# Cross-attention on one core: score tiles of 308, 154 and 154 columns become 234, 234 and 156, and ScalarE writes a second copy of some queries

## The chip, the cores and the metric

One NeuronCore of a Trainium2 chip runs the program. The metric is the time of one execution on the device in microseconds (us), as the median of several; lower is better. The engines are TensorE (PE, with its weight loads shown as PEld), VectorE (DVE), ScalarE (ACT), GpSimd (POOL) and SyncE (SP), which here only issues DMAs. They run side by side, each its own list of instructions in order, and wait for each other through semaphores.

## What is computed

`x` is (32, 512, 640) in fp32, `ctx` is (32, 77, 1024). The reference, cut to what matters (the other key and value weights see empty slices, since all 77 context rows are text):

```
q = heads(x @ to_q_w)            # 20 heads of 32
k, v = heads(ctx @ to_k_w), heads(ctx @ to_v_w)
p = softmax(q @ k.T / sqrt(32))  # 512 x 77 per head
out = merge(p @ v) @ to_out_w + to_out_b + x
```

## The kernel before

**Tiling.** A batch's 640 query columns are five chunks of 128, so a chunk holds four heads of 32 rows. One chunk of one batch is an *item*; there are 32 x 5 = 160. An item's 512 queries are four tiles of 128. Products are made in float32r in three passes: each operand is split into a high part (a cast) and a low part (the rest), and high x high, high x low and low x high are added up in PSUM.

**An item's steps**, each named by one letter in the tables that set the order: `q` (`queries`, 15 matmuls of 512 columns into the one PSUM bank `pq`), `Q` (`high_query`: ScalarE casts `pq` into `qt[:, 0]`), `g` (`low_query`: VectorE subtracts, from `pq` again), `k` (`copy_query`: GpSimd moves rows of `qt` to other partitions), `s` (`score_tile`: three matmuls into one of three `sc` banks), `m` (VectorE: maximum of each head), `e` (`exps`: four exponentials with sums on ScalarE), `N` (normalize, GpSimd), `z` (32x32 block transpose, VectorE), `w` and `d` (out to DRAM and back, which completes the transpose), `c`, `R`, `l` (split of the probabilities), `v` (six matmuls with the values into the one bank pair `pa`), `A`, `a`, `h`, `L` (halves added, split again), `p` (projection, 24 matmuls of 320 columns per item), `f`, `o` (residual added, stored). Loads have `u`: `uk` keys, `uv` values, `ux` and `ur` the input.

**Scores.** A chunk's four heads need twelve products of 32 rows (three for each head) and a matmul takes 128 rows, so three matmuls do it with block-diagonal keys. Before, the first has the high queries of all four heads against 4 x 77 = 308 columns; the second and third have a pair of heads each, 154 columns: low queries against high keys in one half of the rows, high queries (moved there by GpSimd) against low keys in the other. So `qt` holds three stationary tiles `qt[:, 0..2]`. The keys lie in `kb` in four blocks of 154 columns per chunk; SP loads eight pieces per batch and group of chunks (group 0 holds chunks 0 to 2, group 1 chunks 3 and 4), and GpSimd copies two half-blocks (`copy_half_keys`, token `K`) to make the 308-column operand.

**Order.** Nothing is scheduled by the compiler. After a stage that makes all keys and values for 32 x 77 context rows (to about 256 us in the trace), three tables of tokens give the order: `FILL` (the rest of that stage together with batches 0 and 1), `PLAN` (once for each of batches 2 to 30, 29 times) and `LAST_` (batch 31 and the end). A token is chunk digit, letter, argument; every engine runs its share of the tokens in the table's order. Steps of different items are interleaved: the queries of item n+1 stand beside the scores of n and the values of n-4.

**What the change touches**: `score_tile` (L563 to L584), `score_max`, `exps`, `load_keys` and `copy_half_keys` (L503 to L519), `high_query`, `copy_query`, `low_query` (L777 to L787), and the three tables.

## Time and profile before

| | us |
|---|---|
| three timed runs | 1857.3, 1859.1, 1859.61 (median 1859.1) |
| the profiled execution, first to last instruction (the page gives it no other time) | 1856.5 |
| PE busy | 1842.4, 99% of the span |
| ACT busy | 1527.2, 82% |
| DVE busy | 1563.4, 84% |
| POOL busy | 1303.9, 70% |
| DMA: share of the 16 engines on SP's queue | 84.5% |

The shares are means over stages. Up to 256 us only the key and value stage runs, where ACT and POOL have little to do; in the stage of the tables all of them are busier. In a matmul's row the end is modelled and successive matmuls overlap, so what a matmul costs is read from start to start and not from its duration.

### The profile page before, as it was taken

Reading aid. Unit: us, or ns where it says so; the run is one execution under the profiler, and the core shown is the slowest. Engines: PE = TensorE matmul, PEld = TensorE weight load, DVE = VectorE, ACT = ScalarE, POOL = GpSimd, SP = SyncE. Lnnn points to the kernel's source line nnn. Section 1 sums busy time; section 2 is a strip of 40 time slices with the busy share of each in tenths; the row PEclk is TensorE's granted clock in tenths of the full one; section 3 lists DMA queues with packets and bytes.
Section 4 is the critical chain, followed back from the end, with each engine's and each line's share of the span. In section 5 each row is a group of like instructions: output and inputs, shape, how many; then the busy total and the mean of one; then the engine's idle time right before and its main releaser. Section 6 shows DMA issues by size and latency. Waiting matters only on the chain.

```text
span 1856.5 us, 37492 instructions
## 1 busy us (share of the span) xinstructions
PE 1842.4 (99%) x10332; PEld 1655.7 (89%) x10332; DVE 1563.4 (84%) x2502; ACT 1527.2 (82%) x6218; POOL 1303.9 (70%) x1120
## 2 busy tenths in 40 slices
PE   9999999999999999999999999999999999999998
PEld 7888897889999999999999999999999999999998
DVE  5445458899999999999999999999999999999996
ACT  3233248899999999999999999999999999999984
POOL 1100268778788788778778877887778878877874
PEclk9999999999999999999999999999999999999999
DMA  9889779998998898888998888998889988888875
GB/s 188 199 198 249 184 193 256 254 242 235 247 240 243 240 238 232 242 235 236 238 244 237 234 243 237 244 238 237 235 234 244 244 241 236 237 232 243 228 228 187
DMA packets 563296, 431.37 MB, mean 232 GB/s; under 512 B 191120, under 2 KB 471120, under 8 KB 563088
## 3 DMA queue, kind: packets, MB, share of 16 engines
q1 hardware_dynamic: 558192, 413.16, 84.5%
q0 software_dynamic: 4800, 15.65, 2.7%
q8 instruction: 85, 1.39, 0.3%
q14 instruction: 123, 1.01, 0.2%
q10 hardware_dynamic: 96, 0.16, 0.0%
HBM read 247.17 MB, written 181.64 MB: 231 GB/s over the span
## 4 chain that ended last, share of the span: by engine, by line
PE 93%; DMA 4%; SPq 1%; DVE 1%; ACT 1%; issue 0%; POOL 0%; DVEq 0%; ACTq 0%; POOLq 0%
PE po L750 29%; PE pq L542 28%; PE pa L694 12%; PE sc L577 11%; PE pv L204 7%; PE pk L204 6%; DMA pd<-z 1%; DMA cs<-in_ctx_dram 1%; DMA xr<-in_x_dram 1%; DMA wo_s<-wo_dram 0%; DMA wraw<-in_L_xattn_to_v_w_dram 0%; DMA xs<-in_x_dram 0%; DMA wraw<-in_L_xattn_to_k_w_dram 0%; ACT pn L602 0%; DMA raw<-pd 0%
## 5 line engine op out<-in xcount | busy, mean ns | idle before, releaser
L602 ACT ACTIVATE pn<-sc,nm 128x77 f32<-128x77 f32 x2560 | 797.1, 343 | 36.0 <-DVE nm L588 29.6
L750 PE MATMUL po<-wo_s,at 128*128 128x320 f32 x3840 | 707.2, 310 | 0.1
L750 PEld LDWEIGHTS po<-wo_s,at 128*128 128x128 f32 x3840 | 619.7, 188 | 41.1 <-DVE xr L765 0.6
L542 PE MATMUL pq<-xt,wq_s 128*128 128x512 f32 x2400 | 596.7, 394 | 2.9 <-ACT pp L661 1.9
L602 ACT ACTIVATION_READ_ACCUMULATOR pn<-sc,nm 128x1 f32 x2560 | 567.5, 222 | 0.0
L542 PEld LDWEIGHTS pq<-xt,wq_s 128*128 128x128 f32 x2400 | 436.7, 188 | 82.5 <-ACT pp L661 2.1
L617 POOL TENSOR_TENSOR pn<-pn,rs 128x1232 f32<-128x1232 f32 x160 | 389.4, 2434 | 94.0 <-DVE rs L612 90.0
L694 PE MATMUL pa<-pp,vb 128*128 128x512 f32 x960 | 340.9, 403 | 4.1 <-DVE at L731 3.3
L577 PEld LDWEIGHTS sc<-kb,qt 128*128 128x128 f32 x1920 | 302.9, 188 | 14.4 <-ACT pn L602 1.8
L588 DVE TENSOR_REDUCE nm<-sc 128x4 f32<-128x308 f32 x640 | 295.0, 466 | 21.6 <-PE sc L577 16.7
L577 PE MATMUL sc<-kb,qt 128*128 128x154 f32 (+1 forms) x1920 | 301.9, 274 | 0.9 <-ACT pn L602 0.9
L783 POOL CAST qt<-qt 64x512 fp32r<-64x512 f32 x320 | 196.9, 615 | 139.5 <-ACT qt L779 124.4
L712 DVE TENSOR_TENSOR pa<-pa,aw 64x512 f32<-64x512 f32 x320 | 222.3, 695 | 50.4 <-ACT aw L708 43.2
L679 POOL TENSOR_TENSOR pp<-raw,pp 64x512 fp32r<-64x512 f32 x160 | 207.0, 1294 | 66.9 <-ACT pp L661 53.5
L624 DVE STREAM_TRANSPOSE z<-pn 128x1280 f32<-128x1280 f32 x160 | 241.2, 1507 | 8.8 <-DMA pd<-z 3.4
L708 ACT COPY aw<-pa 64x1024 f32<-64x1024 f32 x160 | 162.2, 1014 | 85.0 <-PE pa L694 83.9
L787 DVE TENSOR_TENSOR qt<-pq,qt 64x512 fp32r<-64x512 f32 x320 | 216.8, 678 | 13.9 <-ACT qt L779 9.0
L320 POOL TENSOR_TENSOR xt<-xs,xt 128x512 fp32r<-128x512 f32 x160 | 204.6, 1305 | 20.8 <-ACT xt L316 15.8
L743 POOL TENSOR_TENSOR xr<-xr,bias 128x640 f32<-128x640 f32 x128 | 202.3, 1581 | 13.1 <-issue 3.5
L672 DVE TENSOR_TENSOR pp<-raw,pp 128x1024 fp32r<-128x1024 f32 x160 | 195.7, 1223 | 0.0
L694 PEld LDWEIGHTS pa<-pp,vb 128*128 128x128 f32 x960 | 173.8, 189 | 15.1 <-DVE pp L672 2.3
L663 ACT CAST pp<-raw 128x1024 fp32r<-128x1024 f32 x160 | 168.1, 1051 | 0.7 <-DMA raw<-pd 0.7
(46 smaller groups left out, 1584.2 us busy)
## 6 DMA issues: line engine op xcount, KB each, us to landing
pd<-z SPq DMA_DIRECT2D x640, 160.0 KB, 3.4
raw<-pd SPq DMA_DIRECT2D x160, 512.0 KB, 4.5
xr<-in_x_dram SPq DMA_DIRECT2D x128, 320.0 KB, 3.9
out_dram<-xr SPq DMA_DIRECT2D x127, 320.0 KB, 3.7
xs<-in_x_dram SPq DMA_DIRECT2D x124, 320.0 KB, 5.8
raw<-pd SPq DMA_DIRECT2D x160, 128.0 KB, 4.2
v_dram<-vs SPq DMA_DIRECT2D x80, 192.0 KB, 4.0
k_dram<-ks POOLq DMA_DIRECT2D x20, 512.0 KB, 4.2
```

Of the source, the lines that this page charges most:

```text
L204: nc.tensor.matmul(held[j][:, :gn], w[:, k, a, :], cts[g, k][:, c, :gn], start=(k == 0 and n == 0), stop=(k == NK - 1 and n == 2),)
L542: nc.tensor.matmul(pqs[n], wq_s[:, k, a, j * P : (j + 1) * P], xts[b, k][:, c, :], start=(k == 0 and m == 0), stop=(k == NC_ - 1 and m == 2),)
L577: nc.tensor.matmul(sc[:, cols], qt[:, m, t * P : (t + 1) * P], keys_, start=(m == 0), stop=(m == 2),)
L588: nc.vector.tensor_reduce(nm, sc[:, :KCOLS].rearrange("p (h k) -> p h k", k=NKEY), AX.X, ALU.max, negate=True)
L602: nc.scalar.activation(pnb[n % 2][:, at, :NKEY], sc[:, i * NKEY : (i + 1) * NKEY], AF.Exp, bias=nm[:, i : i + 1], accum_out=sms[n][:, at : ...
L617: nc.gpsimd.tensor_tensor(pf, pf, rs.unsqueeze(2).to_broadcast([P, NQ * HPC, NKEY]), ALU.mult)
L624: nc.vector.transpose(z.rearrange("p b t j -> p t b j"), pn.rearrange("p (t h) k -> p t (h k)", t=NQ).rearrange("p t (b i) -> p t b i", i=Q),)
L679: nc.gpsimd.tensor_tensor(pp[64:, 4, :], raw[:64, 2, :], pp[:64, 4, :].bitcast(F32), ALU.subtract)
L694: nc.tensor.matmul(pas[n][:, p, :], vb[:, p, t, :], pp[:, c, :], start=(c == p), stop=(c == p + 2),)
L712: nc.vector.tensor_tensor(pa[64 * p : 64 * p + 64, 0], pa[:64, p], aw[:, p], ALU.add)
L750: nc.tensor.matmul(pos[b, t, h][:, :HALF], ats[b * NC_ + j][:, a, t * P : (t + 1) * P], wos[0][:, j, c, h * HALF : (h + 1) * HALF], start= ...
L787: nc.vector.tensor_tensor(qt[rows, 1 + w, :], pqs[n][rows], qt[rows, 0, :].bitcast(F32), ALU.subtract)
```

## The change

The twelve products of a chunk are packed evenly: the heads stand in the order 2, 0, 1, 3 in the score bank, each in a block of 78 columns (77 keys and a spare), and the three matmuls cover three blocks (2, 0, 1), three blocks (0, 1, 3) and two blocks (2 and 3, which are the first and the last). So the widths are 234, 234 and 156, 624 columns in place of 616, and the third matmul writes two runs that do not adjoin.

```diff
+KBLK = NKEY + 1
+ORDER = (2, 0, 1, 3)
+WIDTHS = (3 * KBLK, 3 * KBLK, 2 * KBLK)
...
+COPIES = ((1, 0, 0, 0, P), (2, 0, 0, 64, 64), (1, 64, 2, 0, Q))
+LOWS = ((2, 0, 0, P), (0, 96, 32, Q), (1, 64, 0, Q), (2, 64, 64, 64))
...
     def score_tile(n, t):
...
-        for m, (cols, keys_) in enumerate(
-            (
-                (slice(0, KCOLS), kb[:, 0::3, jg]),
-                (slice(0, half), kb[:, 1, jg]),
-                (slice(half, KCOLS), kb[:, 2, jg]),
-            )
-        ):
+        blocks = score_blocks(sc)
+        for m, heads in enumerate((blocks[:, 0:3], blocks[:, 1:4], blocks[:, 0::3])):
+            c0 = keys_at(nj, m) + (j - j0) * WIDTHS[m]
             nc.tensor.matmul(
-                sc[:, cols],
+                heads,
                 qt[:, m, t * P : (t + 1) * P],
-                keys_,
+                kb[:, c0 : c0 + WIDTHS[m]].rearrange("p (h k) -> p h k", k=KBLK),
...
-    def high_query(n):
+    def high_query(n, m=0):
         open_first()
-        nc.scalar.copy(qts[n % 2][:, 0, :], pqs[n])
+        nc.scalar.copy(qts[n % 2][:, m, :], pqs[n])
 
     def copy_query(n, w):
-        qt, half = qts[n % 2], (slice(0, 64), slice(64, P))
-        nc.gpsimd.tensor_copy(qt[half[1 - w], 1 + w, :], qt[half[w], 0, :].bitcast(F32))
+        qt, (m1, r1, m0, r0, rn) = qts[n % 2], COPIES[w]
+        nc.gpsimd.tensor_copy(qt[r1 : r1 + rn, m1, :], qt[r0 : r0 + rn, m0, :].bitcast(F32))
 
     def low_query(n, w):
-        qt, rows = qts[n % 2], slice(64 * w, 64 * w + 64)
-        nc.vector.tensor_tensor(qt[rows, 1 + w, :], pqs[n][rows], qt[rows, 0, :].bitcast(F32), ALU.subtract)
+        qt, (m1, r1, r0, rn) = qts[n % 2], LOWS[w]
+        rows = slice(r0, r0 + rn)
+        nc.vector.tensor_tensor(
+            qt[r1 : r1 + rn, m1, :], pqs[n][rows], qt[rows, 0, :].bitcast(F32), ALU.subtract
+        )
...
-        elif op == "K":
-            copy_half_keys(*arg)
+        elif op == "B":
+            high_query(n + 1, 1)
```

**Queries.** The first stationary tile is all high queries but for rows 96 to 127, which become the low queries of head 1 (`g1`, 32 rows). The second is all high queries but for rows 64 to 95, the low queries of head 0. The third has the high queries of heads 2 and 3 in rows 0 to 63 (`k1`) and low queries below. `k1` reads the rows that `g1` overwrites, so `g1` has to come after it, and `g1` is now the last reader of `pq`. There are two ways to fill the second and third tile. In most items of `PLAN`: `k0` (GpSimd copies all 128 rows of high queries), `g0` (VectorE, all 128 low rows into the third tile), `k2` (GpSimd takes 32 low rows from there), `k1`, `g1`. In `FILL`, `LAST_` and, for `k0` alone, one item of `PLAN` in five: token `B`, in which ScalarE casts `pq` a second time, into the second tile; in `FILL` and `LAST_` VectorE then makes the low rows in three subtractions (`g3`, `g2`, `g1`), and GpSimd is left with `k1`. The item behind `PLAN`'s token 3 has `k0`, `k1` and the three subtractions.

**Keys.** GpSimd's copies (`K`) go. SP loads ten pieces per batch and group in place of eight; two of the ten carry both the high and the low part.

```diff
-    def load_keys(b, g, heads=range(HPC), parts=(0, 1)):
...
-                    nc.sync.dma_start(kb[rows, 1 + i // 2, :, half], src[own, part])
...
+    def load_head_keys(b, g, piece):
+        nj = GROUPS[g][1]
+        i, part, quad, m, block = KEYS_OF[piece]
...
+        nc.sync.dma_start(
+            dst[:, c0 : c0 + nn * w].rearrange("p (r k) -> p r k", k=w)[:, :, :NKEY],
+            src[:, n0 : n0 + nn, b * NKEY : (b + 1) * NKEY].bitcast(F32),
+        )
```

**Order.** `FILL` and `LAST_` keep their old order with the new tokens in the old places; `PLAN` is another order altogether. Two lines of it, the start:

```diff
     PLAN = (
-        "1uv10 0r 0e0 0s2 0ux3 0g0 0N 0v0 1uv15 0v1 0m1 0v2 0f10 0p16 1uv11 0e1 0v4 0g1 0uk120 0p17 0v3 "
+        "0r 0v0 0v1 1uv10 0uk12 1uv16 0g0 0m1 0v2 0s2 0m2 0v3 0f10 0ux3 0v4 1uv15 0k0 0p16 0e0 1uv14 0k2 "
```

On TensorE, in the first batches of `PLAN`, two score tiles stand next to each other behind a projection (`po`) and are followed by another. Before:

```order
L750 MATMUL po<-wo_s,at_2694 128x320 x3
L577 MATMUL sc<-kb_1753,qt_1920 128x308
L577 MATMUL sc<-kb_1753,qt_1920 128x154 x2
L577 MATMUL sc<-kb_1753,qt_1920 128x308
L577 MATMUL sc<-kb_1753,qt_1920 128x154 x2
L750 MATMUL po<-wo_s,at_2689 128x320 x3
```

The same engine after, with the same surroundings (`128x2x78` is the third matmul, two runs of 78 columns):

```order
L745 MATMUL po<-wo_s,at_2698 128x320 x3
L577 MATMUL sc<-kb_1753,qt_1921 128x234 x2
L577 MATMUL sc<-kb_1753,qt_1921 128x2x78
L577 MATMUL sc<-kb_1753,qt_1921 128x234 x2
L577 MATMUL sc<-kb_1753,qt_1921 128x2x78
L745 MATMUL po<-wo_s,at_2699 128x320 x3
```

Each tile keeps three matmuls; their widths are what moved.

On GpSimd, the part of a `PLAN` batch that ends with the normalize (`pn`), last probabilities (`pp`) and low inputs (`xt`) ahead of the fourth item's query copies. Before:

```order
L617 TENSOR_TENSOR pn_1921<-pn_1921,rs 128x16x77
L679 TENSOR_TENSOR pp<-raw,pp 64x512
L320 TENSOR_TENSOR xt<-xs,xt 128x512
L783 CAST qt_1919<-qt_1919 64x512 x2
L320 TENSOR_TENSOR xt<-xs,xt 128x512 x4
L679 TENSOR_TENSOR pp<-raw,pp 64x512
L617 TENSOR_TENSOR pn_1922<-pn_1922,rs 128x16x77
L743 TENSOR_TENSOR xr<-xr,bias 128x640
L783 CAST qt_1920<-qt_1920 64x512
L519 CAST kb_1753<-kb_1753 64x462 x2
L783 CAST qt_1920<-qt_1920 64x512
```

After:

```order
L612 TENSOR_TENSOR pn_1923<-pn_1923,rs 128x16x77
L674 TENSOR_TENSOR pp<-raw,pp 64x512
L345 TENSOR_TENSOR xt<-xs,xt 128x512
L778 CAST qt_1921<-qt_1921 128x512
L778 CAST qt_1921<-qt_1921 64x512
L345 TENSOR_TENSOR xt<-xs,xt 128x512 x3
L738 TENSOR_TENSOR xr<-xr,bias 128x640
L674 TENSOR_TENSOR pp<-raw,pp 64x512
L778 CAST qt_1920<-qt_1920 128x512
L778 CAST qt_1920<-qt_1920 32x512
L778 CAST qt_1920<-qt_1920 64x512
```

The copies of keys are gone, the fifth item has three query copies where it had two, and the copies stand in the order `k0`, `k2`, `k1`.

On ScalarE, the start of `FILL`'s attention part, where the first items' queries are cast between other casts of the key stage. Before:

```order
L225 CAST ks<-pk 128x416
L779 CAST qt_1919<-pq 128x512
L316 CAST xt<-xs 128x512
L225 CAST ks<-pk 128x416 x2
L779 CAST qt_1920<-pq 128x512
```

After:

```order
L250 CAST ks<-pk 128x416
L774 CAST qt_1920<-pq 128x512 x2
L341 CAST xt<-xs 128x512
L250 CAST ks<-pk 128x416 x2
L774 CAST qt_1921<-pq 128x512 x2
```

Every cast of `pq` is there twice, one behind the other, and the exponentials that follow stand behind both.

More of the change, by code (lines that the diff above doesn't have):

```diff
@@ L452, in open_small @@
             small = ctx.enter_context(tc.tile_pool(name="small", bufs=1, reuse_waits="tile"))
-            kbs.append(small.tile([P, 4, GROUPS[0][1], KCOLS // 2], FPR, name="kb0"))
+            kbs.append(small.tile([P, keys_width(GROUPS[0][1])], FPR, name="kb0"))
     def open_first():
@@ L548, in queries, with score_blocks @@
                 )
-    def split_q(n):
-        qt, pq = qts[n % 2], pqs.pop(n)
-        nc.scalar.copy(qt[:, 0, :], pq)
-        lower, upper = slice(0, 64), slice(64, P)
-        halves = ((lower, upper), (upper, lower))
-        for w, (r, other) in enumerate(halves):
-            nc.gpsimd.tensor_copy(qt[other, 1 + w, :], qt[r, 0, :].bitcast(F32))
-        for w, (r, other) in enumerate(halves):
-            nc.vector.tensor_tensor(
-                qt[r, 1 + w, :], pq[r], qt[r, 0, :].bitcast(F32), ALU.subtract
-            )
+    def score_blocks(sc):
+        return sc[:, : HPC * KBLK].rearrange("p (h k) -> p h k", k=KBLK)
     def score_tile(n, t):
@@ L599, in exps @@
             sms[n] = small.tile([P, NQ * HPC], F32, tag="sm", name="sm", bufs=2)
-        for i in range(HPC):
-            at = t * HPC + i
+        for i, head in enumerate(ORDER):
+            at = t * HPC + head
             nc.scalar.activation(
                 pnb[n % 2][:, at, :NKEY],
-                sc[:, i * NKEY : (i + 1) * NKEY],
+                sc[:, i * KBLK : i * KBLK + NKEY],
                 AF.Exp,
```

52 lines of the change are left out of this document (26 added, 26 removed), and 164 rows, old and new, of tables (FILL, LAST_, PLAN).

## The prediction

> **What bounds the kernel now.** I read the page's shares and chain first, then the stretches of the span, then single rows of TensorE around one score tile. The page:
>
> ```profile
> span 1856.5 us, 37492 instructions
> PE 1842.4 (99%) x10332; PEld 1655.7 (89%) x10332; DVE 1563.4 (84%) x2502; ACT 1527.2 (82%) x6218; POOL 1303.9 (70%) x1120
> PE 93%; DMA 4%; SPq 1%; DVE 1%; ACT 1%; issue 0%; POOL 0%; DVEq 0%; ACTq 0%; POOLq 0%
> ```
>
> TensorE carries 93% of the chain that ended last. The shares are means, so the stretches (each: length, then busy us and count of PE, PEld, DVE, ACT, POOL; then clock, DMA share, GB/s):
>
> ```profile
> 260.00:340.00 80.00, 74.99 (x389) 65.31 (x389) 61.64 (x98) 68.25 (x307) 67.19 (x69) 1.00 0.89 237
> 310.00:330.00 20.00, 16.91 (x82) 13.18 (x80) 16.44 (x26) 19.90 (x93) 15.36 (x15) 1.00 0.97 304
> 370.00:390.00 20.00, 19.37 (x110) 17.10 (x110) 18.60 (x28) 19.02 (x73) 16.65 (x14) 1.00 0.84 231
> 1140.00:1240.00 100.00, 100.00 (x584) 91.04 (x583) 91.86 (x147) 92.14 (x386) 80.52 (x70) 1.00 0.90 239
> 1740.00:1857.00 117.00, 111.10 (x664) 101.75 (x662) 91.86 (x146) 84.74 (x320) 75.29 (x57) 1.00 0.70 208
> ```
>
> In the steady stretch (1140 to 1240, all of it PLAN) TensorE never stands; VectorE, ScalarE and the DMAs follow at about 92, 92 and 90 in 100. A batch has 285 matmuls (75 queries, 120 projections, 30 values, 60 scores), so it lasts 285/584 x 100 = 48.8 us. Only in FILL does TensorE stand: ScalarE is busy 19.90 of 20 at 310 to 330, and 5.0 us of TensorE are lost between 260 and 340. So in PLAN a shorter matmul stream is a shorter batch; in FILL more work on ScalarE is more time.
>
> A busy TensorE hides what its matmuls wait for. One score tile, in single rows (start, duration), read in narrow windows; PEld are the weight loads:
>
> ```profile
> 1000.15 1.48 PE L750 MATMUL po<-wo_s,at 128*128 128x320 f32 x9
> 1001.47 0.49 PE L577 MATMUL sc<-kb,qt 128*128 128x308 f32 x3
> ...
> 1001.47 0.33 PEld L577 LDWEIGHTS sc<-kb,qt 128*128 128x128 f32 x2
> 1001.61 0.19 PEld L577 LDWEIGHTS sc<-kb,qt 128*128 128x128 f32 x1
> 1001.72 0.19 PEld L694 LDWEIGHTS pa<-pp,vb 128*128 128x128 f32 x1
> 1001.83 0.19 PEld L750 LDWEIGHTS po<-wo_s,at 128*128 128x128 f32 x1
> ...
> 1001.60 0.35 PE L577 MATMUL sc<-kb,qt 128*128 128x154 f32 x2
> 1001.67 0.28 PE L577 MATMUL sc<-kb,qt 128*128 128x154 f32 x1
> ...
> 1006.61 3.65 PE L542 MATMUL pq<-xt,wq_s 128*128 128x512 f32 x15
> 1010.10 0.60 PE L750 MATMUL po<-wo_s,at 128*128 128x320 f32 x3
> ```
>
> The load for the second matmul starts with the first matmul (1001.47), the next at 1001.61 with the second, and then loads follow each other by 0.11, whether the matmul between them is long or not. So a load takes 0.11 and there is one spare place for weights: a matmul of 154 columns streams in 0.07 (1001.60 to 1001.67) but costs 0.11, because the weights of the next one are not there. From load to load the tile costs 0.14 + 0.11 + 0.11 = 0.36 us (1001.47 to 1001.83). Long matmuls cover their loads: nine of 320 columns take 1.32, 0.147 each, fifteen of 512 take 3.49, 0.233 each.
>
> **The change part by part.** *Widths.* Between 320 and 512 columns a column costs (0.233 - 0.147)/192 = 0.00045 us, so 234 columns take 0.147 - 86 x 0.00045 = 0.108, just what a load takes (0.11). 156 columns stream in about 0.07 and are bound by the load. The tile then costs 0.11 + 0.11 + 0.11 = 0.33, 0.03 less, though it has eight columns more. Bounds: not under 0.33, since no loads stand closer; not over 0.14 + 0.14 + 0.11 = 0.39, since 234 columns can't take longer than the 308 do. I take 0.33, the interpolation's value; 0.345 if load and stream, now equally long, miss each other by 0.007 twice. PLAN has 29 x 20 = 580 tiles: 580 x 0.03 = 17.4 us.
>
> The Trainium skill (TensorE: Matmul & The Clock Gate, "LDWEIGHTS (loading the stationary operand)" and "Back-to-back issue gap") gives a load 128/1.2 = 107 ns and a matmul N/2.4 + 2.5 ns, which makes the tile 131 + 107 + 107 = 345 ns before and 3 x 107 = 321 after, 24 ns less. By that estimate PLAN would gain 13.9 us; the trace agrees on the load (0.11) and has the 308 columns at 0.14.
>
> *ScalarE, VectorE, GpSimd in PLAN.* The prices:
>
> ```profile
> L779 ACT CAST qt<-pq 128x512 fp32r<-128x512 f32 x123 | 73.1, 594 | 0.4
> L787 DVE TENSOR_TENSOR qt<-pq,qt 64x512 fp32r<-64x512 f32 x246 | 166.4, 677 | 3.7
> L731 DVE TENSOR_TENSOR at<-pa,at 128x512 fp32r<-128x512 f32 x123 | 84.8, 690 | 34.0 <-ACT at L726 32.2
> L617 POOL TENSOR_TENSOR pn<-pn,rs 128x1232 f32<-128x1232 f32 x123 | 299.3, 2433 | 66.6 <-DVE rs L612 63.0 <-DMA pd<-z 3.5
> L679 POOL TENSOR_TENSOR pp<-raw,pp 64x512 fp32r<-64x512 f32 x123 | 159.2, 1295 | 48.8 <-ACT pp L661 43.1
> L320 POOL TENSOR_TENSOR xt<-xs,xt 128x512 fp32r<-128x512 f32 x120 | 152.4, 1298 | 3.8
> L783 POOL CAST qt<-qt 64x512 fp32r<-64x512 f32 x246 | 150.3, 611 | 108.2 <-ACT qt L779 96.5
> L519 POOL CAST kb<-kb 64x308 fp32r<-64x308 f32 (+1 forms) x98 | 49.6, 506 | 6.5 <-DMA kb<-k_dram 0.7
> ```
>
> 64 or 128 partitions cost the same on both engines (677 against 690, 1295 against 1298), so I price every subtraction at 0.68 and every query copy at 0.61, whatever its rows. ScalarE gets one cast per batch, 0.59; VectorE eleven subtractions in place of ten, 0.68; GpSimd thirteen query copies in place of ten and no key copies, 3 x 0.61 - 4 x 0.51 = -0.2. In a batch that shrinks from 48.8 to 48.2 ScalarE then has 0.921 x 48.8 + 0.6 = 45.6 us of work and VectorE 0.919 x 48.8 + 0.7 = 45.5, 94 to 95%. Both stay under TensorE, so I charge nothing; the cover is the 2.6 us that is left, and it is thinner.
>
> *The wait that is new.* `pq` is one bank; the next item's queries wait for its last reader. That was a subtraction behind the cast. Now it is `g1`, behind `k1` on GpSimd, mostly behind `k0` and `k2`: cast, copy, copy, copy, subtraction, 0.59 + 3 x 0.61 + 0.68 = 3.1 us. While `g1` waits, VectorE's later maxima and transposes stand behind it. The shortest cover in the new table lies between the token `3q4` and the token `4q0`: six projection steps, six value matmuls and a score tile, 6 x 3 x 0.147 + 6 x 0.233 + 0.33 = 4.4 us. There the chain is without `k2`, 0.59 + 2 x 0.61 + 0.68 = 2.5, so 1.9 are left. I take no stall.
>
> *SP and the DMAs.* Four loads more per batch; two of each ten are of double size:
>
> ```profile
> 1002.90 0.43 SPq L512 DMA_DIRECT2D kb<-k_dram  x1
> ...
> kb<-k_dram SPq DMA_DIRECT2D x256, 28.9 KB, 3.0
> ...
> kb<-k_dram SPq DMA_DIRECT2D x256, 19.2 KB, 3.2
> ```
>
> 4 x 0.43 = 1.7 us more of SP's queue, which issues some 74 in 48.8 us, and 4 x (28.9 + 19.2) = 192 KB more, 0.8 us at 239 GB/s: the DMA share goes from 0.90 to about 0.93. In the new table the last keys of a batch (`3uk07`) stand behind the store `4o0`, which waits for the projection step `4p8`. From there to the first score that needs them (`5s0`) TensorE has five projection steps, five value matmuls, two score tiles and five query steps, 5 x 0.44 + 5 x 0.233 + 2 x 0.33 + 5 x 0.70 = 7.5 us, against 3.0 for landing. Nothing charged.
>
> *FILL and LAST.* Here ScalarE gets a cast (0.59) and VectorE a subtraction (0.68) per item, on an old order. Eleven items in FILL: at worst all of it in series, 11 x 1.27 = 14; at best nothing. TensorE stands only in about 100 of FILL's 150 us, some six items: I charge the cast there, 6 x 0.59 = 3.6, less 40 x 0.03 = 1.2 gained: +2.4. In LAST ScalarE waits for the value matmuls often enough to hide it:
>
> ```profile
> ACT aw L708 <- PE pa L694: 14.3, 9, 3.4
> ```
>
> That is 14.3 us in nine waits from 1745 on, against 3 x 0.59; zero there, and up to +2.
>
> *Sum*: 1856.5 - 17.4 + 2.4 = 1841.5 for the profiled execution. The median of the runs stands 2.6 above that span (1859.1), so 1844.
>
> **The rivals.** *Half the gain*: the tie of load and stream costs 0.007 per wide matmul (tile 0.345), or the thinner cover of ScalarE and VectorE lets a wait through. 580 x 0.015 = 8.7 gained, 2.4 + 2.6 added: 1852.8. For it: two engines at 95%; against: at 92% not one wait reaches TensorE in the steady stretch.
>
> *The split output is slow*: the third matmul writes two runs of 78 columns, which no row shows. If that halves its rate it streams in 2 x 0.07 = 0.14, the tile is 0.11 + 0.11 + 0.14 = 0.36, nothing is gained and FILL's 3.6 stay: 1862.7. It decides once the third matmul takes over 0.11, a loss of the whole 0.03 at 0.14. Against: the 308 columns read their keys in two runs and keep to the line (0.147 - 12 x 0.00045 = 0.142). The Trainium skill (PSUM — Partial Sum Buffer, "Specifications (TRN2)") says that any non-contiguous access pattern slows matmuls significantly; by that rule this rival holds. No run here shows it for an output.
>
> *`pq` comes free late*, the rival on the slower side: in GpSimd's order a normalize (2.43), a `pp` (1.30) and an `xt` (1.30) stand right ahead of the fourth item's copies. If GpSimd reaches `k0` more than 1.9 us after the cast, the queries of token `4q0` wait. One `xt` too late in each batch is 29 x 1.30 = 37.7: 1856.5 - 17.4 + 2.4 + 37.7 + 2.6 = 1881.8; from 0.55 us per batch on the gain is gone. For it: GpSimd is the one engine that `pq` did not depend on. Against: its idle time ahead of its query copies is mostly waiting for the cast (96.5 of 108.2 us), so it is early there.
>
> *No effect*: the loads of the neighbours, not the tile, set the 0.36, and TensorE's stream is as long as before: 1859 to 1861.
>
> **How the numbers follow.** Forecast 0.64 (1837 to 1850, its own range), half the gain 0.17, split output 0.07, late `pq` 0.08, no effect 0.04. A measurement here tells 0.2% (3.7 us: 1855.4 to 1862.8) from no change. Faster: the forecast and most of the second, 0.79. Same: no effect, half of the split output and the rest of the second, 0.09. Slower: late `pq` and the other half, 0.12. The range for 8 in 10 holds the first two: from 1837 (rows are rounded to 0.01, so a tile may gain 0.035; 640 x 0.035 = 22.4 with nothing lost in FILL: 1856.5 - 22.4 + 2.6 = 1836.7) to 1858, the far side of the second.
>
> **What would show it.** In the profile after, weight loads around a score tile at steps of 0.11, none of 0.14, and 1140 to 1240 with about 591 matmuls (584 x 48.8/48.2) and a full TensorE. A step of 0.14 behind the third matmul is the split output. A wait of `pq`'s matmuls for VectorE's `qt` in every batch is the late bank. The stretch 260 to 390 should be some 2 us longer. I am wrong if PLAN's batch is not near 48.2 us, and in the mechanism if it is but the steps of the loads are not 0.11.

## The result and the profile after

The kernel after takes 1921.6 us (median of 4 runs, 1920.6 to 1922.0) against 1858.7 for the kernel before: a ratio of 1.0338, 95% interval 1.0323 to 1.0352. It is 63 us slower where 15 less were forecast, outside the range and beyond every rival's time. The page of the profiled execution, the lines that answer to those of before:

```profile
span 1918.8 us, 37409 instructions
PE 1852.6 (97%) x10332; PEld 1640.0 (85%) x10332; DVE 1614.2 (84%) x2546; ACT 1554.3 (81%) x6261; POOL 1387.9 (72%) x1065
PE 32%; DVE 26%; DMA 11%; ACT 9%; POOL 8%; SPq 7%; issue 7%; POOLq 0%; DVEq 0%; ACTq 0%
```

The shares of busy time hardly moved (TensorE 99 to 97%). The third line, the chain that ended last, tells more: it was 93% TensorE's, and now it runs through every engine. The stretches (length; busy us and count of PE, PEld, DVE, ACT, POOL; clock, DMA share, GB/s):

```profile
260.00:340.00 80.00, 66.92 (x345) 57.56 (x344) 60.67 (x95) 64.16 (x289) 50.60 (x49) 1.00 0.86 217
310.00:330.00 20.00, 13.36 (x69) 10.89 (x68) 18.09 (x30) 19.31 (x79) 13.09 (x11) 1.00 0.84 246
1140.00:1240.00 100.00, 97.76 (x568) 87.53 (x567) 91.84 (x147) 91.45 (x382) 84.72 (x64) 1.00 0.87 237
```

The steady stretch (1140 to 1240) has 568 matmuls where 591 were foretold (584 before), and TensorE stands for 2.2 of 100 us. The first matmul of each batch, found in the trace, gives the loss by stage:

| stage | before, us | after, us | difference |
|---|---|---|---|
| up to PLAN (FILL's stage) | 351.5 | 368.1 | +16.6 |
| PLAN, 29 batches | 1423.0 | 1460.6 | +37.6 |
| LAST_ to the end | 82.0 | 90.2 | +8.2 |
| median batch of PLAN | 48.99 | 50.28 | +1.29 |

**The tile did what was foretold.** One score tile in narrow windows, as before:

```profile
1001.34 0.19 PEld L577 LDWEIGHTS sc<-kb,qt 128*128 128x128 f32 x1
1001.34 0.27 PE L577 MATMUL sc<-kb,qt 128*128 128x234 f32 x1
...
1001.45 0.19 PEld L577 LDWEIGHTS sc<-kb,qt 128*128 128x128 f32 x1
1001.56 0.19 PEld L745 LDWEIGHTS po<-wo_s,at 128*128 128x128 f32 x1
```

The loads follow the first matmul at 0.11 and again 0.11 (1001.34, 1001.45, 1001.56); the step of 0.14 is gone, and from 450 to 1740, over 513 tiles, the median from a tile's second load, which starts with its first matmul, to the second load behind the tile is 331 ns against 363. So PLAN lost 1.29 + 0.6 us per batch somewhere else. Two waits stand in it where there were none (TensorE, 450 to 1740 us: who waits for whom, us in total, times, longest):

```profile
PE pa L689 <- DVE at L726: 20.9, 27, 0.8
PE sc L577 <- DVE qt L783: 8.7, 25, 0.8
```

Both are once per batch: a value matmul (token `3v0`) behind VectorE's `3L`, and a score tile (`2s0`) behind the low queries `1g1`. Neither is a wait that the prediction priced. What makes them late is in the groups by shape (GpSimd and VectorE, 450 to 1740; busy us, mean ns | idle before):

```profile
L778 POOL CAST qt<-qt 32x512 fp32r<-32x512 f32 x103 | 106.2, 1031 | 27.5 <-DVE qt L783 25.1 <-DVE xr L760 0.6
L778 POOL CAST qt<-qt 128x512 fp32r<-128x512 f32 x103 | 84.9, 824 | 69.3 <-ACT qt L774 65.2
L778 POOL CAST qt<-qt 64x512 fp32r<-64x512 f32 x128 | 78.2, 611 | 8.1
L667 DVE TENSOR_TENSOR pp<-raw,pp 128x1024 fp32r<-128x1024 f32 x129 | 179.6, 1392 | 3.7
```

Of before, the same subtraction of VectorE, the token `R`, which makes the low parts of the weights (`rest_p`):

```profile
L672 DVE TENSOR_TENSOR pp<-raw,pp 128x1024 fp32r<-128x1024 f32 x132 | 158.6, 1201 | 0.0
```

A GpSimd copy of 32 rows lasts 1.03 us on the mean and one of 64 rows 0.61: rows can't be the reason. `R` is longer too, 1.39 for 1.20. Side by side in one batch of after (start, duration; `1R`, the copies `1k2` and `1k1` in one row, `1g1`; then `3l`, `3R`, `2x1`, `3L` and the value matmul):

```profile
984.58 1.22 DVE L667 TENSOR_TENSOR pp<-raw,pp 128x1024 fp32r<-128x1024 f32 x1
984.82 2.11 POOL L778 CAST qt<-qt 32x512 fp32r<-32x512 f32 x2 [0.70 <-DVE qt L783]
986.96 0.69 DVE L783 TENSOR_TENSOR qt<-pq,qt 32x512 fp32r<-32x512 f32 x1 [0.78 <-POOL qt L778]
987.79 0.35 PE L577 MATMUL sc<-kb,qt 128*128 128x234 f32 x1 [0.30 <-DVE qt L783]
...
1002.98 1.28 POOL L674 TENSOR_TENSOR pp<-raw,pp 64x512 fp32r<-64x512 f32 x1
1003.62 1.73 DVE L667 TENSOR_TENSOR pp<-raw,pp 128x1024 fp32r<-128x1024 f32 x1
1004.34 2.14 POOL L345 TENSOR_TENSOR xt<-xs,xt 128x512 fp32r<-128x512 f32 x1
1005.66 0.68 DVE L726 TENSOR_TENSOR at<-pa,at 128x512 fp32r<-128x512 f32 x1
1006.39 0.72 PE L689 MATMUL pa<-pp,vb 128*128 128x512 f32 x2 [0.75 <-DVE at L726]
```

In the first group `R` runs from 984.58 to 985.80; the two copies, the first of which starts inside it, need 2.11 us in place of 1.22, the subtraction waits 0.78 for them, the score tile 0.30 for the subtraction. In the second, `R` starts while GpSimd's `3l` runs and lasts 1.73, and the `xt` that starts inside `R` lasts 2.14 (1.30 alone); `3L` stands behind `R` on VectorE, the value matmul behind `3L`. Before, of all five `R` of a batch only one met GpSimd's work for more than 0.1 us: a normalize (from 980.89, with `R` from 980.66), which lasted 3.06 in place of 2.28 and for which no matmul waited.

**FILL and LAST_** show the mechanism of the rival "late `pq`", in the stages where the prediction did not look for it (TensorE, 250 to 372 before, the same of after, then 1830 to the end of after; before has no such wait there):

```profile
PE pq L542 <- DVE qt L787: 0.9, 1, 0.9
```
```profile
PE pq L557 <- DVE qt L783: 12.4, 7, 3.2
```
```profile
PE pq L557 <- DVE qt L783: 3.5, 2, 2.4
```

The query matmuls wait for the last subtraction that reads `pq`. Around three of these waits the granted clock fell (the stretch 350 to 370, then eleven of the twelve query matmuls behind a wait of 2.05 us):

```profile
350.00:370.00 20.00, 18.46 (x88) 15.65 (x87) 16.60 (x25) 14.91 (x65) 10.46 (x8) 0.84 0.86 230
```
```profile
348.76 4.25 PE L557 MATMUL pq<-xt,wq_s 128*128 128x512 f32 x11
```

Eleven matmuls took 4.25 us; in the prediction's row fifteen took 3.65. In the trace of after the granted clock is 0.50 for 3.41 us three times, from 349.40, 359.64 and 1834.20. At half the clock that is at most 1.7 us of lost work each, by estimate 3.4 us of FILL's 16.6 and 1.7 of LAST_'s 8.2. TensorE's idle time from 250 to PLAN went from 5.1 to 17.4 us, so idle time and clock together make FILL's loss up. In LAST_ the waits for `pq` are 3.5 of some 6 us of added idle time.

### The profile page after: what moved, and what is told of

Read it like the earlier page. It is cut to its first block, busy times and chain, and to the rows that moved or that the text cites. A ratio compares the mean times of both kernels' runs of the same rounds, so it can differ in the third digit from the quotient of the medians.

```text
span 1918.8 us, 37409 instructions
## 1 busy us (share of the span) xinstructions
PE 1852.6 (97%) x10332; PEld 1640.0 (85%) x10332; DVE 1614.2 (84%) x2546; ACT 1554.3 (81%) x6261; POOL 1387.9 (72%) x1065
## 4 chain that ended last, share of the span: by engine, by line
PE 32%; DVE 26%; DMA 11%; ACT 9%; POOL 8%; SPq 7%; issue 7%; POOLq 0%; DVEq 0%; ACTq 0%
PE pq L557 7%; PE po L745 7%; PE pk L229 6%; PE pv L229 6%; DVE z L619 5%; DVE pa L707 5%; ACT pn L597 5%; PE pa L689 4%; POOL qt L778 4%; POOL pn L612 4%; DVE nm L589 4%; DVE pp L667 3%; DVE qt L783 3%; DVE xr L760 3%; PE sc L577 2%
## 5 line engine op out<-in xcount | busy, mean ns | idle before, releaser
L745 PE MATMUL po<-wo_s,at 128*128 128x320 f32 x3840 | 672.3, 311 | 0.1
L557 PE MATMUL pq<-xt,wq_s 128*128 128x512 f32 x2400 | 636.6, 399 | 15.9 <-DVE qt L783 15.9
L597 ACT ACTIVATION_READ_ACCUMULATOR pn<-sc,nm 128x1 f32 x2560 | 597.0, 235 | 0.0
L778 POOL CAST qt<-qt 64x512 fp32r<-64x512 f32 (+2 forms) x393 | 314.7, 801 | 137.0 <-ACT qt L774 91.0
L689 PE MATMUL pa<-pp,vb 128*128 128x512 f32 x960 | 299.6, 404 | 29.6 <-DVE at L726 26.1
L783 DVE TENSOR_TENSOR qt<-pq,qt 32x512 fp32r<-32x512 f32 (+2 forms) x364 | 247.6, 680 | 84.0 <-POOL qt L778 46.6
L589 DVE TENSOR_REDUCE nm<-sc 128x4 f32<-128x308 f32 x640 | 289.2, 465 | 12.4 <-PE sc L577 8.2
L577 PE MATMUL sc<-kb,qt 128*128 128x234 f32 (+1 forms) x1920 | 284.4, 265 | 13.6 <-DVE qt L783 12.0
L674 POOL TENSOR_TENSOR pp<-raw,pp 64x512 fp32r<-64x512 f32 x160 | 239.5, 1497 | 32.5 <-ACT pp L656 16.5
L345 POOL TENSOR_TENSOR xt<-xs,xt 128x512 fp32r<-128x512 f32 x160 | 229.9, 1454 | 24.6 <-ACT xt L341 19.7
L667 DVE TENSOR_TENSOR pp<-raw,pp 128x1024 fp32r<-128x1024 f32 x160 | 222.6, 1391 | 4.2
```

Of the source, the lines that this page charges most:

```text
L557: nc.tensor.matmul(pqs[n], wq_s[:, k, a, j * P : (j + 1) * P], xts[b, k][:, c, :], start=(k == 0 and m == 0), stop=(k == NC_ - 1 and m == 2),)
L577: nc.tensor.matmul(heads, qt[:, m, t * P : (t + 1) * P], kb[:, c0 : c0 + WIDTHS[m]].rearrange("p (h k) -> p h k", k=KBLK), start=(m == 0), ...
L589: nc.vector.tensor_reduce(nm, score_blocks(sc)[:, :, :NKEY], AX.X, ALU.max, negate=True)
L597: nc.scalar.activation(pnb[n % 2][:, at, :NKEY], sc[:, i * KBLK : i * KBLK + NKEY], AF.Exp, bias=nm[:, i : i + 1], accum_out=sms[n][:, at ...
L667: nc.vector.tensor_tensor(pp[:, 2:4, :], raw[:, 0:2, :], pp[:, 0:2, :].bitcast(F32), ALU.subtract)
L689: nc.tensor.matmul(pas[n][:, p, :], vb[:, p, t, :], pp[:, c, :], start=(c == p), stop=(c == p + 2),)
```

## The experiments

Every time is the median of a timed comparison; "after" is 1921.6, "before" about 1859. Stage times are from each profile's trace, as in the table.

### What takes PLAN's time

**R with one input in SBUF** (`r_one_input`). Edit:

```diff
-        nc.vector.tensor_tensor(
-            pp[:, 2:4, :], raw[:, 0:2, :], pp[:, 0:2, :].bitcast(F32), ALU.subtract
-        )
+        high = pp[:, 0:2, :].bitcast(F32).rearrange("p a (s k) -> p a s k", k=1)
+        nc.vector.tensor_reduce(pp[:, 2:4, :], high, AX.X, ALU.max)
```

> The kernel after, with VectorE's rest of the weights (token R, a subtraction of two tiles in SBUF, 128x1024) replaced by a reduction over groups of one element that reads the cast tile alone: same columns, one input in SBUF. The low parts of the weights are left out of the result. Theory A (while R runs, GpSimd's copies stand, and R stands while GpSimd runs; in the new order R meets the copies k2 and k0, which last 1.44 to 1.48 us in place of 0.61, and the chain to g1 and to the value matmuls is late): the copies last 0.61 again, R is 1.1 to 1.2 everywhere, the wait before the value matmul 3v0 (0.98 us per batch) goes, and most of the 0.47 before the score tile 2s0; the batch falls from 50.28 by 1.0 to 1.5 us, the whole by 29 to 44: 1878 to 1893 us. Theory B (the chain cast, k0, k2, k1, g1 is too long by itself, whatever R does): the copies get shorter, the batch does not by more than 0.2 us: 1916 to 1922. Theory C (ScalarE, with one more cast per batch, is what ends the waits): likewise 1916 to 1922. The Trainium skill (SBUF - State Buffer, Who interferes with whom) says that a VectorE instruction with two inputs in SBUF contends with a GpSimd instruction that reads SBUF, and that a reduction never does; by that sentence theory A's first half holds.

Measured: 1871.4 us, 50 less than after, beyond the larger bound of theory A. The copies of 32 rows, though `R` runs beside two of four as in after:

```profile
L777 POOL CAST qt<-qt 32x512 fp32r<-32x512 f32 x106 | 64.3, 607 | 42.0 <-DVE qt L782 38.3 <-DVE xr L759 0.8
```

The batch is 48.49, PLAN 1413.7, 46.9 less than after and 9.3 less than before; the two waits of once per batch are gone from TensorE. Theory A holds; B and C fall for PLAN. The Trainium skill (SBUF — State Buffer, "Who interferes with whom") says that a VectorE instruction with two inputs in SBUF contends with a GpSimd instruction that reads SBUF, and that a reduction never does: the trace agrees, 1.03 us against 0.61.

**The control** (`before_one_input`): the same edit in the kernel before.

> The control to r_one_input: the kernel before, with the same reduction in place of R (the low parts of the weights are left out). Theory A (R and GpSimd exclude each other, and only the new order lets them meet where TensorE waits): in before only 4N meets R (3.06 us against 2.28) and TensorE never stands in PLAN, so nothing changes by more than 4 us: 1855 to 1861, and the new tiles are worth about 0.5 us per batch (48.49 against 48.99) without R. Theory D (R costs every order about the same, and the 50 us gained there are not the change's): 1810 to 1830 us.

Measured: 1857.2 us, ratio to before 0.9988 (0.9978 to 0.9997); the batch stays 48.99. Theory D falls: `R`'s second input cost the old order nothing that reaches the total.

**R with one input in two items of five** (`one_input_13`). Edit: the reduction where `2 <= b < B - 1 and j in (1, 3)`, the subtraction elsewhere.

> The kernel after, with the reduction in place of R in PLAN's items 1 and 3 alone, ahead of the two places where TensorE waits (the score tile 2s0 and the value matmul 3v0); R of items 0, 2 and 4 stays a subtraction and goes on meeting k2, k0 and l (the low parts of two items in five are left out). Theory A in its narrow form (only the meetings ahead of the two waits cost anything): the batch falls to 48.5 to 48.8, the whole to 1870 to 1880. In its wide form (each meeting makes the next engine late, and the wait moves to another place): 49.2 to 49.8, 1890 to 1907.

Measured: 1892.4 us, batch 49.04. The whole lies in the range of the wide form, the batch between the two: PLAN falls from 1460.6 to 1430.5, 30.1 of the 46.9. The meetings ahead of the two waits cost most, not all.

**R in two halves** (`r_halves`). Edit: `for a in range(2)` around the subtraction, each of 128x512.

> The kernel after, with R as two subtractions of 128x512 in place of one of 128x1024. Theory A (GpSimd is held for as long as one instruction of VectorE lasts, and may start between two): a copy that met R is held for at most 0.6 us in place of 0.87, and the batch falls by 0.2 to 0.8 us, the whole to 1897 to 1916; if VectorE's second half takes the place first, nothing changes, 1918 to 1925.

Measured: 1955.0 us, 33 slower than after. A miss, in the direction too:

```profile
L668 DVE TENSOR_TENSOR pp<-raw,pp 128x512 fp32r<-128x512 f32 x252 | 235.8, 974 | 3.5
```

Two halves last 2 x 0.97 = 1.95 us where the whole lasted 1.39. The copies of 32 rows do get shorter (0.77 on the mean), but `R`'s halves now wait for GpSimd as well, and TensorE's wait for `3L` behind them grows from 20.9 to 40.2 us.

**The old order** (`old_order`). Edit: PLAN's table is that of before; a line of it, old and new:

```diff
-0m2 0p20 0k0 1uv17 0z 0v5 0s3 0k1 0A 1q0
+0m2 0p20 1uv17 0z 0v5 0s3 0A 1q0
```

(`0k0`, `0g0`, `0k2`, `0k1` stand together ahead of `0N`, `0g1` behind them; likewise the others, but for the one item with `B`, which has three subtractions and `k1`; the key copies `K` are dropped, each key load is one or two of the new pieces.)

> The kernel after, with PLAN in the order of the kernel before: the steps stand as they stood, the key loads in the new pieces, the copies of keys dropped, and the query steps put in as k0 behind the cast, k2 and k1 behind g0, g1 behind k1. FILL and LAST are untouched. Theory A (it is the new order that puts R onto GpSimd's copies, and the score tile gains 0.03 us as measured): the batch is 48.4 to 49.3 us against 50.28, the whole 1867 to 1893. Theory B (the longer chain of copies in any order makes pq late, and the new order was needed for it): the batch is 50 us or longer, 1915 or more.

Measured: 2042.2 us, batch 54.5. Here `R` lasts 1.22 and every query copy 0.61, so neither lengthens the other, and yet it is the slowest of all. TensorE, 450 to 1740:

```profile
PE sc L577 <- DVE qt L783: 23.3, 24, 1.0
PE pa L689 <- POOL pp L674: 22.8, 23, 1.0
PE po L745 <- DVE xr L760: 17.7, 23, 0.8
PE pq L557 <- DVE qt L783: 16.6, 24, 0.7
```

Theory B holds for this order: the chain of copies makes scores and `pq` late in it. So the new order was of use: with the same chain its batch is 4.2 us shorter, and it pays by putting `R` onto GpSimd's work. My substitution is one of many, and says nothing of a better one.

**Another query form** (`form_d`). Edit: the cast goes to the second tile, which both subtractions then read, so that nothing overwrites what a copy still needs before `pq` is free:

```diff
-COPIES = ((1, 0, 0, 0, P), (2, 0, 0, 64, 64), (1, 64, 2, 0, Q))
-LOWS = ((2, 0, 0, P), (0, 96, 32, Q), (1, 64, 0, Q), (2, 64, 64, 64))
+COPIES = ((0, 0, 1, 0, 96), (1, 64, 2, 0, Q), (2, 0, 0, 64, Q), (2, 32, 1, 96, Q))
+LOWS = ((2, 0, 0, P), (0, 96, 32, Q))
```

All three tables in the order of before, `k1` `k2` `k3` at the second copy's place.

> The score tiles and key loads of the kernel after, all three tables in the order of the kernel before, and the query steps in another form: the cast writes the second query tile, both subtractions read it and pq and stand where they stood, the first copy (96 rows) at the old first copy's place, and three copies of 32 rows at the second's; no second cast. So pq is freed by cast and two subtractions, as in before, and no subtraction waits for GpSimd, which has four copies per item. Theory A (the loss is the price of the new chain, through its order in PLAN and through pq in FILL and LAST; the tile's 0.03 us are real): the batch is 48.3 to 48.9 us, FILL and LAST stand within 3 us of before, the whole 1837 to 1856. Theory B (any form with more than two copies per item is late, wherever pq is freed): the batch is over 49.5 us, the whole over 1875. Theory C (ScalarE's second cast made FILL long): FILL is back within 3 us of before, LAST too, whatever PLAN does.

Measured: 1955.8 us: PLAN's batch 51.99, FILL's stage 359.0, LAST_ 83.0. For PLAN theory B's numbers hold: 40.5 us of waits of score tiles for GpSimd's copies between 450 and 1740. But `R` meets GpSimd's work here too (four of five per batch, 1.59 us on the mean), so how much of that is the number of copies is not shown. For the ends theory A does better: LAST_ is back within 1 us of before, FILL has got back 9 of its 16.6.

### What takes FILL and LAST_

**No second cast** (`fl_copies`). Edit, in FILL and LAST_ only: `B` becomes `k0`, `g3` becomes `g0`, `k1` becomes `k2 k1`, `g2` is dropped.

> The kernel after, where the first two batches and the last split their queries as the steady batches do: no second cast on ScalarE, but GpSimd copies k0, k2, k1 and two subtractions (g0, g1) in place of three. PLAN is untouched. FILL is 16.6 us longer than before the change and LAST 8.2. Theory A (ScalarE's second cast costs it, in a stretch where ScalarE is full): 15 to 20 of the 24.8 come back, 1902 to 1907 us. Theory B (the bank pq is freed late, by the subtraction g1 behind GpSimd's copy k1; now behind three copies): FILL and LAST get no shorter, or longer by up to 2 us per item in 11 + 4 items: 1920 to 1945.

Measured: 1930.2 us, FILL's stage 374.2, LAST_ 92.7. ScalarE has less to do and the ends are 8.6 us longer; theory A (here: ScalarE's cast) falls as the main cause, theory B holds. What the cast costs by itself can't be read here, since the copies that replace it cost at the same time.

**g1 free of GpSimd** (`fl_split`). Edit, in FILL and LAST_ only: `k1` becomes `k3 k4`, with `(2, 0, 0, 64, Q), (2, 32, 1, 96, Q)` added to `COPIES`.

> The kernel after, where in the first two batches and the last the copy k1 of 64 rows is made as two copies of 32 rows (k3 from the first query tile, k4 from the second), so that neither reads the rows that the subtraction g1 overwrites: g1, which frees pq, no longer waits for GpSimd. ScalarE's two casts and VectorE's three subtractions stay; GpSimd has 0.61 us more per item. PLAN is untouched. Theory B (pq late behind k1): the waits of the query matmuls for VectorE's qt, 12.4 us in seven places of FILL, go, and with the clock that falls behind them FILL and LAST lose 15 to 20 of their 24.8: 1902 to 1907 us. Theory A (ScalarE's second cast): at most 3 us come back: 1918 to 1922.

Measured: 1917.4 us, FILL's stage 364.3, LAST_ 86.2: 7.8 us less in the ends (and PLAN 2.7 longer, 1.7 of it in its first batch). The whole lies in neither range, just under theory A's. The ends go the way of theory B, by half of its size: the chain is then cast, three subtractions, no shorter than 0.59 + 3 x 0.68 = 2.6 us, and 7.8 of the 12.4 us of waits stay.

**The ends in form D** (`d_ends`). Edit: FILL and LAST_ as in `form_d`, PLAN as in after. The first item of LAST_ is cast in PLAN, so it keeps PLAN's form (`k0`, `g0`, `k2`, `k1`, `g1`).

> PLAN of the kernel after untouched; the first two batches and the last in the order of the kernel before with the query form of form_d (pq freed by the cast and two subtractions, none behind GpSimd; four copies per item). Theory B of the ends (what made FILL and LAST long is how late pq is freed: the query form) expects what form_d showed in these stages, FILL 9 us and LAST 7 us shorter than after, and PLAN as in after (1460): the whole 1903 to 1908 us. If form_d's ends were short only because its PLAN left them otherwise, 1915 to 1922.

Measured: 1910.8 us: FILL's stage 359.0 as in `form_d`, LAST_ 87.1 (not 83), PLAN 1462.6. FILL's 9 us come back whatever PLAN follows; the whole is 3 us above theory B's range. LAST_ got back 3.1 us where it got back 7.2 in `form_d`: the queries behind its first item, which has the old chain, wait 2.2 us for `pq`.

**One subtraction** (`ends_one_sub`). Edit: in `d_ends` the low rows of `g1` come by a fifth copy, `(0, 96, 2, 32, Q)`, and `g1` is dropped.

> d_ends, where VectorE makes one subtraction per item in the first two batches and the last: the low part of the second head goes by a fifth GpSimd copy. pq is then free after cast and one subtraction, 0.59 + 0.68 = 1.27 us, in place of 1.95. Theory B (the chain to pq alone sets FILL): the remaining waits for VectorE's qt in FILL (2.5 us) go, FILL is 2 to 7 us shorter than in d_ends: 1896 to 1903. Theory G (what is left of FILL is GpSimd, whose copies come too late for the scores): FILL and LAST are 3 to 8 us longer, with more waits of the score tiles for GpSimd's qt: 1907 to 1915.

Measured: 1914.2 us (the profiled execution took 1918.2), FILL's stage 363.9. The waits of FILL's stage (250 to 372), first in `fl_copies` (its window runs to 376), `fl_split`, `d_ends`, then here:

```profile
PE pq L557 <- DVE qt L783: 13.9, 6, 3.6
```
```profile
PE pq L557 <- DVE qt L783: 7.8, 5, 2.9
```
```profile
PE sc L580 <- POOL qt L781: 3.0, 5, 1.0
PE pq L560 <- DVE qt L786: 2.5, 2, 1.3
```
```profile
PE sc L580 <- POOL qt L781: 7.2, 10, 1.1
...
PE pq L560 <- DVE qt L786: 0.4, 2, 0.2
```

With the chain from the cast to the free bank the waits for `qt` of VectorE fall: three copies and a subtraction (13.9), one copy among three subtractions (12.4, the kernel after), three subtractions (7.8), two (2.5), one (0.4). But each copy more on GpSimd makes the scores wait, 7.2 us with five. Theory G holds for what is left: in each of these forms either `pq` or the scores are late in FILL.

**Both causes taken away** (`d_ends_one_input`): `d_ends` with the reduction in place of `R`.

> d_ends with R as the reduction with one input in SBUF (the low parts of the weights are left out). If the 62 us are the sum of two causes, R against GpSimd's copies in PLAN (46.9 us between the PLANs of after and r_one_input) and the late pq in FILL and LAST (16), both taken away give 1918.8 - 46.9 - 16 = 1856 for the span, 1855 to 1860 us for the median, with a batch of 48.5. If they overlap, or a third cause is in it, 1865 or more. The longer FILL of 7 us that GpSimd's four copies leave is in this number.

Measured: 1859.1 us, span 1855.5, batch 48.49, ratio to before 1.0003 (0.9993 to 1.0012). The 62 us over the kernel before are covered by these two causes to 1 us. It is a balance: PLAN is 9.1 us under before, the ends are still 8.2 over it. To the forecast span of 1841.5 another 14 us are missing, 8 of them in PLAN and the rest in the ends.

### What the tile is worth

**The tile alone** (`tiles_alone`). Edit to the kernel before:

```diff
-                (slice(0, KCOLS), kb[:, 0::3, jg]),
-                (slice(0, half), kb[:, 1, jg]),
-                (slice(half, KCOLS), kb[:, 2, jg]),
+                (blocks[:, 0:3], kb[:, 0:3, jg, :78]),
+                (blocks[:, 1:4], kb[:, 1:4, jg, :78]),
+                (blocks[:, 0::3], kb[:, 1:3, jg, :78]),
```

> The kernel before in every order, load, copy and subtraction, with the columns of its three score matmuls alone changed to 234, 234 and 156 (the third into two runs of 78); they read other columns of the keys than the reference asks for, so the scores are left wrong. It is the prediction's first term by itself. Theory A (the tile is worth 0.03 us, and the rest of the change lost it): load steps of 0.11 three times, a batch of 48.35 us against 48.99, 29 batches and some 60 tiles outside PLAN: 17 to 19 us less, 1839 to 1843. Theory H (half the gain: at 94 to 95% of VectorE and ScalarE a shorter stream lets their waits through): 1846 to 1853. Theory N (the neighbours set the pace, or the waits take all of it): 1856 to 1861.

Measured: 1855.7 us, ratio to before 0.9974 (0.9965 to 0.9983), batch 48.90. Theory N is the nearest, and yet the loads stand at 0.11: some 13 of the 17 us are missing. Where they went, in one tile per batch (`4k0`, `5R`, then the tile `5s0`, whose second matmul waits):

```profile
986.57 2.16 POOL L785 CAST qt<-qt 64x512 fp32r<-64x512 f32 x1
987.05 1.21 DVE L674 TENSOR_TENSOR pp<-raw,pp 128x1024 fp32r<-128x1024 f32 x1
988.18 0.19 PEld L578 LDWEIGHTS sc<-kb,qt 128*128 128x128 f32 x1
988.32 0.27 PE L578 MATMUL sc<-kb,qt 128*128 128x234 f32 x1
...
988.79 0.63 PEld L578 LDWEIGHTS sc<-kb,qt 128*128 128x128 f32 x5 [0.42 <-POOL qt L785]
```

The same two instructions in the kernel before:

```profile
1036.48 0.61 POOL L783 CAST qt<-qt 64x512 fp32r<-64x512 f32 x1
1037.09 1.21 DVE L672 TENSOR_TENSOR pp<-raw,pp 128x1024 fp32r<-128x1024 f32 x1
```

There `R` begins at 1037.09, as the copy ends. In the shorter batch it begins 0.48 us after the copy's start, the copy lasts 2.16, and the score tile pays.

**The tile alone, R with one input** (`tiles_one_input`) and **with the copy earlier** (`tiles_k_early`, `4k0` ahead of `4K00` and `4K01`):

> tiles_alone with R as the reduction with one input in SBUF (beside the scores, the low parts of the weights are left wrong). In tiles_alone the stream was shorter by 0.026 us per tile where nothing waits, but in one tile of each batch (5s0) the second matmul waits 0.36 us for GpSimd's copy 4k0, which lasts 2.15 us because VectorE's 5R now starts 0.5 us after it, where in before it started as the copy ended. Theory A (R's meeting with that copy took the gain): the copy lasts 0.61, the batch is 48.3 to 48.5 us, the whole 1841 to 1846. Theory S (a stream that is shorter by so little meets the next late engine at once): 1850 or more.

> tiles_alone with R as it is, and GpSimd's copy 4k0 one place earlier, ahead of the two key copies 4K00 and 4K01, so that it has ended before 5R starts (5R then begins at about the end of 4K01, or holds it up). Theory A: the wait of 0.36 us goes, and the batch falls to 48.4 to 48.6, the whole to 1843 to 1849, with R unchanged. If the key copy that meets R is as urgent as the query copy was, or it was not the meeting, 1853 to 1857.

Measured: 1841.4 us with one input (0.9905, 0.9890 to 0.9920), batch 48.45; 1853.8 with the copy earlier (0.9975, 0.9965 to 0.9984), batch 48.85. Theory A in the first; in the second its other branch, since the key copy that now meets `R` is as urgent (TensorE, 450 to 1740):

```profile
PE sc L578 <- POOL kb L519: 4.2, 27, 0.2
```

**R as it is, the bias sum later** (`tiles_b_late`). Edit: in `tiles_alone` the token `4b1` moves behind `4k0`.

```diff
-4o0 4p10 4b1 4p11 4g1
+4o0 4p10 4p11 4g1
...
-4k0 4e3
+4k0 4b1 4e3
```

> tiles_alone with R as it is and GpSimd's bias sum 4b1 (1.57 us) behind the copies of item 4 in place of ahead of them. The copies 4k1, 4K00, 4K01, 4k0 then end some 1.5 us earlier, and 5R should start at about the end of 4b1, so that it meets nothing that a score tile waits for. Theory A: no wait in the tile 5s0, a batch of 48.4 to 48.6 us and the whole at 1841 to 1847, with R unchanged and the same work in every engine. Theory S (the next late engine is met at once, wherever R stands): 1851 to 1857.

Measured: 1841.8 us, ratio to before 0.9899 (0.9882 to 0.9915), batch 48.44. The copy, the bias sum and `R`, then the steady stretch:

```profile
978.62 0.61 POOL L785 CAST qt<-qt 64x512 fp32r<-64x512 f32 x1
979.31 1.56 POOL L745 TENSOR_TENSOR xr<-xr,bias 128x640 f32<-128x640 f32 x1
980.63 1.32 DVE L674 TENSOR_TENSOR pp<-raw,pp 128x1024 fp32r<-128x1024 f32 x1
```
```profile
1140.00:1240.00 100.00, 100.00 (x592) 90.92 (x591) 92.72 (x149) 93.11 (x398) 81.43 (x71) 1.00 0.90 243
```

Every engine runs the same instructions as in `tiles_alone`; one token of GpSimd stands elsewhere. Here the copy is both undisturbed and earlier; in `tiles_one_input` it stayed where it was, and the whole is the same. So the 14 us between `tiles_alone` and these two are the meeting of `R` with one copy, shown once by `R`'s inputs and once without touching `R`. A version that beats the kernel before was not found: the faster ones leave parts of the scores or the weights out, and the tile needs one of the new query forms, of which the best here (`d_ends`) stands at 1910.8.

## Why the prediction was wrong

- **What bounds the kernel**: right. TensorE set PLAN's end and any shorter stream is a shorter batch, as long as nothing waits. The batch before is 48.99 us, by the first matmul of each, where 48.8 was worked out; so 48.44 in `tiles_b_late` is the 48.2 of the forecast.
- **Widths** (0.36 to 0.33 per tile, 17.4 us in PLAN): right, with no part lost to the split output. From the starts of all matmuls of 23 batches a tile's three matmuls took 332 ns before and 306 in `r_one_input`, 26 less; the estimate from the Trainium skill (TensorE: Matmul & The Clock Gate, "LDWEIGHTS (loading the stationary operand)" and "Back-to-back issue gap") gave 24 and the rows 30. PLAN went from 1423.0 to 1405.7, 17.3 less, in `tiles_b_late`. That this meets 17.4 is in part luck: 580 tiles at 26 ns are 15.1, and the first batch of PLAN is 1.8 shorter (it is 1.5 shorter in `before_one_input` too, where no tile changed). The whole of `tiles_b_late`, 1841.8, and its 592 matmuls in the steady stretch are close to what was forecast for the change. It was the forecast of the tile alone.
- **ScalarE, VectorE, GpSimd in PLAN: the step that failed.** "I price every subtraction at 0.68 and every query copy at 0.61, whatever its rows ... Both stay under TensorE, so I charge nothing". The sums of two engines were about right (VectorE 46.2 and ScalarE 46.0 us per batch, where 45.5 and 45.6 were written); GpSimd's was not: 42.6 against 39.4 before, where 0.2 less was written, and 38.3 in `r_one_input`. Wrong was that the price of a step holds wherever it stands: the table moves `R` onto GpSimd's copies, which then last up to 1.48 (mean of 32 rows 1.03), `R` 1.39, and two waits per batch reach TensorE. Term charged: 0. Term measured: 46.9 us of PLAN, the difference between after and `r_one_input`.
- **The new wait on `pq`** ("I take no stall"): right at the place it named, between `3q4` and `4q0` of PLAN, where TensorE never waited for it. The chain that it priced did cost time, in another stage.
- **FILL and LAST** (+2.4 and 0): wrong by their size, and in the main for another reason than ScalarE's cast. They measured +16.6 and +8.2. In FILL most of it is the chain to `pq`, 12.4 us of waits, and up to 3.4 of the clock; in LAST_ the chain's waits are 3.5 and the clock's share up to 1.7. The runs took back only part of the 24.8: `d_ends` 12.2 in all. The prediction had late `pq` as a rival with its mechanism, but tried it on PLAN's cover of 4.4 us alone; in FILL's old order the waits show that the cover is shorter than the chain.
- **SP and the DMAs** (nothing charged): right. At a full stream with the new key loads, in `d_ends_one_input` from 1140 to 1240, the DMA share is 0.90 as before, not 0.93; TensorE waited for key loads three times between 375 and 1775 there, 1.2 us in all.
- **The rivals**: half the gain, split output and no effect did not happen. For the split output, the load behind the third matmul came 0.11 after the one before it, so the slowing by a non-contiguous output that the prediction set beside this rival was not seen. Late `pq` happened, in FILL and LAST_. The one that decided, that `R` and GpSimd's operations lengthen each other where the order lets them meet, was not among them. A trace of before shows it only in its single rows: four of five normalizes last 2.28 us, the one beside `R` 3.06, and the prediction read the mean, 2.43.
- **What stays open.** With `R` on one input the new PLAN gains 9.3 us, not 17.3. Its usual batch has nearly all of the gain (48.49, against 48.44 in `tiles_b_late`). Most of the rest lies in a few longer batches, 7.6 us in sum over the usual one where `tiles_b_late` has 0.9: the first is 2.7 longer, the ninth 2.1 with a value matmul that waits 1.7, the 26th 1.2 with two waits for key loads. Why was not tried. What makes the half of the ends that `d_ends` did not take back is known only in part (the waits for GpSimd's copies). Whether an order exists that carries the new query form and keeps `R` off the copies is open too.

## What to carry to other kernels

Where an order is rewritten, look for the pairs that lengthen each other (here a VectorE operation with two inputs in SBUF, and GpSimd's copies) and see where the new order lets them meet before pricing anything by its mean: a duration is a property of a place. When a local gain disappears, look for the one instruction that changed its length, and try to move something else; a single token of GpSimd was worth 14 us here. And price a changed chain in every stage that runs it, first in the one with the least cover.

## What the runs showed of the hardware

- Beside VectorE's subtraction of two SBUF tiles, GpSimd's operations that read SBUF last longer than alone: a copy up to 1.55 us (2.16 for 0.61), a normalize 0.78 (3.06 for 2.28). The subtraction itself is longer beside some of GpSimd's (1.73 for 1.20). A reduction of the same size with one SBUF input did not do this: in `r_one_input` the copies beside it last 0.61.
- It was not always the one that started first that kept its length: by the profile's spans, in `tiles_alone` the copy had run 0.48 of its 0.61 us when `R` began, `R` took its usual 1.21, and the copy ended 0.47 after it. Halving `R` did not help: in `r_halves` its two halves last 1.95 together, where the whole lasted 1.39.
- In after the granted clock was 0.50 for 3.41 us three times, from within 1 us of the end of waits of 2.05, 1.14 and 2.42 us (0.84 on the mean of 350 to 370). Behind the longest waits, 2.90 us up to 316.46 and 3.17 up to 326.90, it stayed at 1.00.
- A matmul whose output is two runs that do not adjoin (156 columns) delayed no weight load: the loads around it follow at 0.11.
